# Feed-forward weights in 48 pieces, the first self-attention projections inside the feed-forward, and the gated weights' scaling kept at its place in the program

## The chip, the cores and the metric

The kernel runs on one core of a Trainium2 chip. Its time is the device time of one execution in microseconds (us). Engines are called PE (TensorE, matrix products), DVE (VectorE), ACT (ScalarE), POOL (GpSimd) and SP (SyncE, which here only issues DMAs). Each works through its own queue in order.

## The reference

A decoder of two layers over 16 sequences of 128 tokens with 512 features, every step followed by a residual sum and a layernorm. What matters here are the end of the first layer and the first half of the second:

```python
# end of layer 0: feed-forward with ternary weights (hidden size 2048)
xq = activation_quant(rms_norm(x))                      # rounded to 8 bit
p = silu(xq @ sign(W_g).T) * (xq @ sign(W_u).T)
x = layernorm(x + p @ sign(W_d).T)
# layer 1: self attention, all four products quantised (16 heads of 32, 4 key heads, rope, causal)
x = layernorm(x + bitlinear_attention(x))
# layer 1: gated cross attention on 128 context tokens
xn = rmsnorm(x) * norm_w
x = layernorm(x + sigmoid(xn @ wg.T) * (attention(xn @ wq.T, ctx) @ wo.T))
```

Before them come a state-space scan and a cross attention, behind them a mixture of experts.

## The kernel before

Five stages run one after the other in the source: `stage_ssm`, `stage_xattn`, `stage_ffn`, `stage_attention`, `stage_moe`. The tile framework traces them, orders the instructions of each engine by a priority (their place in the program) with a cost model of its own, and puts in the waits; an instruction can be issued far ahead of its place when its inputs and its buffer are there. `keep_in_program_order` forbids this for one instruction. Inside a stage the order is written by hand: helpers are generators, a list `running` holds those under way, and each step of a stage's loop advances each of them by one `yield`.

Large weights live in five slots of 16 KB per partition (`k.wslot`). In cross attention all five are full: two halves of wq, wk and wv together, two halves of wo (eight heads each).

`stage_xattn` loops over 128 units (16 sequences, 4 key groups, 2 halves). A unit makes scores, exponentials, transposes; `project(b)` runs eleven units ahead and uses the tiles `xT` and `cT`, two buffers each, 2 KB per partition. `prepare_first` quantises the feed-forward's first two sequences at the end.

`load_ffn_weights` is called where `stage_ffn` begins. For gate and up it brings two raw halves of 2 MB each into slots and takes their signs (ACT) into one bfloat16 slot; for down, two raw halves and two slots of signs.

`stage_ffn` takes two sequences at a time (`states`, eight of them). For a sequence and each quarter h of the hidden size it makes gate and up products, Silu (ACT), their product (DVE), a transpose, a split into a high and a low part (`hi`, `lo`) and eight products into `po`. `late`, `nxt` and `ahead` are generators advanced between: the last layernorm, the next two sequences' quantisation, and the preparation of attention's weights and masks (`load_bit_weights`, `load_gated_masks`).

`stage_attention` has 16 pairs of sequences, eight of `SelfAttention` and eight of `GatedAttention`, eight units each. A `SelfAttention` pair first runs `project()`, in twelve steps: `levels` (the rows' largest value, scaling, rounding, transposes), key and value product `pkv`, rope on keys (`kr`, whose addition and scaling run on POOL), query products `pq` and their rope (`qr`, addition on POOL), transposes. Pair 0's twelve steps and five of pair 1's are written ahead of the loop. In the loop, units run through scores, maximum (DVE), exponentials (ACT), row sums (`at_h`, `at_p` on POOL) and transposes.

`load_gated_weights` brings wq, wg, wo of the gated attention when `stage_attention` begins, waits eight steps, and multiplies the four chunks of wq and of wg by the norm's weights on POOL (line 870), a chunk every second step of the program.

Of the kernel before, what the change touches and what calls it, by code (L numbers as in the profile page):

```python
# [10 lines left out]
F32 = mybir.dt.float32  # L11
BF16 = mybir.dt.bfloat16
F32R = mybir.dt.float32r
# [7 lines left out]
P = 128  # L21
# [6 lines left out]

class Ctx:
    pass  # L30


class Side:
# [3 lines left out]
    def __init__(self, k):  # L37
        self.tc, self.n = k.tc, 0
# [375 lines left out]
def stage_xattn(k):  # L414
# [9 lines left out]
    with ExitStack() as ctx:  # L424
# [200 lines left out]

        def prepare_first():

            homes = {"xn": (wk, "m1", 4), "q_t": (wk, "m2", 2), "q_q": (wk, "sq", 2), "pt": (ppt, "pt", 2), "q_T": (k.early, "q_T0", 2)}
            st = k.ffn_first = Ctx()
            st.xs = k.x[0:2]  # L630

            def new(what, shape, dt):
                pool, tag, bufs = homes[what]
                return pool.tile(shape, dt, tag=tag, name=what, bufs=bufs)

            return prepare_ffn(k, st, new)

        def advance():
            for job in list(running):
                if next(job, running) is running:  # L640
                    running.remove(job)

        units = [(b, g, i) for b in range(NB) for g in range(G) for i in range(2)]
        running = [clear_rows(k, cst)]
        for t in range(-12, len(units) + 4):
            for lag, what in ((3, turn), (2, norm), (1, exps), (0, top), (-1, scores)):
                if not 0 <= t - lag < len(units):
                    continue
                b, g, i = units[t - lag]
                st = state[b]  # L650
                if what is scores and (g, i) == (0, 0):
                    st.b, st.sc, st.mx, st.pr, st.sm, st.pTs = b, {}, {}, {}, {}, {}
                what(st, g, i)
                if what is turn and i == 1:
                    running.append(outputs(st, g))
            if t == len(units) - 4:
                running.append(prepare_first())
            b, r = divmod(t + 11, U)
            if r == 0 and b < NB:
                running.append(project(b))  # L660
            b, r = divmod(t + 15, U)
            if t == -12 or r == 0 and b > 0 and b < NB and b % 4 == 0:
                running.append(angles(max(b, 0) // 4))
            advance()
# [1 line left out]
            advance()  # L666


def load_ffn_weights(k):

    nc, a = k.nc, k.args
    k.fw = []
    for name in ("ff_wgT", "ff_wuT"):
        wb = None
        for i in range(2):
            raw = k.wslot()
            nc.sync.dma_start(
                raw.rearrange("p (c e) -> p c e", c=2), a[name][i * 256 : (i + 1) * 256].rearrange("(c p) e -> p c e", p=P)
            )
            if wb is None:  # L680
                wb = k.wslot(BF16)
            for c in range(4):
                nc.scalar.activation(wb[:, i * 4096 + c * 1024 : i * 4096 + (c + 1) * 1024], raw[:, c * 1024 : (c + 1) * 1024], AF.Sign)
        k.fw.append(wb.rearrange("p (c e) -> p c e", c=KC))
    k.fd = []
    for i in range(2):
        raw = k.wslot()
        nc.sync.dma_start(
            raw.rearrange("p (h e) -> p h e", h=8), a["ff_wdT"][i * 1024 : (i + 1) * 1024].rearrange("(h p) e -> p h e", p=P)
        )  # L690
        fd = k.wslot(F32R)
        for c in range(4):
            nc.scalar.activation(fd[:, c * 1024 : (c + 1) * 1024], raw[:, c * 1024 : (c + 1) * 1024], AF.Sign)
        k.fd.append(fd.rearrange("p (h e) -> p h e", h=8))


def prepare_ffn(k, st, new):
# [31 lines left out]
def stage_ffn(k):  # L729
# [4 lines left out]
    with ExitStack() as ctx:  # L734
# [2 lines left out]
        pp = ctx.enter_context(tc.tile_pool(name="s3p", bufs=2, space=PSUM))  # L737
        po_ = ctx.enter_context(tc.tile_pool(name="s3o", bufs=1, space=PSUM))
        raws = ctx.enter_context(tc.tile_pool(name="s3r", bufs=1))
        load_ffn_weights(k)  # L740
        ahead = chain(load_bit_weights(k, raws, po_), load_gated_masks(k, raws))

        def prepare(st):
# [5 lines left out]
        def finish(st):  # L749
            layernorm(k, st.xs, st.xs)  # L750
            yield

        states = []
        for b0 in range(0, NB, 2):
            st = Ctx() if b0 else k.ffn_first
            st.xs = k.x[b0 : b0 + 2]
            states.append(st)
        late = iter(())
        for n, sn in enumerate(states):
            nxt = prepare(states[n + 1]) if n + 1 < len(states) else iter(())  # L760
            for i, x in enumerate(sn.xs):
                st = sn.step[:, i : i + 1]
                po = po_.tile([P, D], F32, tag="po", name="po")
                for h in range(HB):
                    ps = []
                    for w, tag in zip(k.fw, ("pg", "pu")):
                        p = pg.tile([P, D], F32, tag=tag, name=tag)
                        for c in range(KC):
                            nc.tensor.matmul(p, sn.qT[i][:, c], w[:, c, h * D : (h + 1) * D], start=c == 0, stop=c == KC - 1)
                        ps.append(p)  # L770
                    sg = wk.tile([P, D], F32, tag="sg", name="sg")
                    nc.scalar.activation(sg, ps[0], AF.Silu, scale=st)
                    nc.vector.scalar_tensor_tensor(sg, ps[1], st, sg, ALU.mult, ALU.mult)
                    pt = pp.tile([P, D], F32, tag="pt", name="pt")
                    transpose4(k, pt, sg)
                    hi = wk.tile([P, D], F32R, tag="hi", name="hi")
                    lo = wk.tile([P, D], F32R, tag="lo", name="lo")
                    nc.scalar.copy(hi, pt)
                    nc.vector.tensor_tensor(lo, pt, hi, ALU.subtract)
                    for part in (hi, lo):  # L780
                        for c in range(4):
                            hc = 4 * h + c
                            nc.tensor.matmul(
                                po, part[:, c * P : (c + 1) * P], k.fd[hc // 8][:, hc % 8],
                                start=part is hi and hc == 0, stop=part is lo and hc == 15,
                            )
                    next(late, None)
                    next(nxt, None)
                    if n and h >= 2:
                        next(ahead, None)  # L790
                nc.vector.tensor_tensor(x, po, x, ALU.add)
            late = finish(sn)
        for _ in late:
            pass


# [60 lines left out]
def load_gated_weights(k):  # L857

    nc, a, pool = k.nc, k.args, k.gated_pool
    W = k.gated_w = {}  # L860
    nw = pool.tile([P, KC], F32, name="nw")
    nc.sync.dma_start(nw, a["x2_nw"].rearrange("(c p) -> p c", p=P))
    for n in ("wq", "wg", "wo"):
        W[n] = pool.tile([P, KC, D], F32, name="x2_" + n)
        nc.sync.dma_start(W[n], a["x2_" + n + "T"].rearrange("(c p) e -> p c e", p=P))
    for _ in range(8):
        yield
    for n in ("wq", "wg"):
        for c in range(KC):
            nc.gpsimd.tensor_scalar(W[n][:, c], W[n][:, c], nw[:, c : c + 1], None, ALU.mult)  # L870
            yield
            yield


class SelfAttention:
# [8 lines left out]

    def __init__(self, k, p, pools):
        self.k, self.nc, self.xs = k, k.nc, k.x[2 * p : 2 * p + 2]
        self.wk, self.wr, self.pp, self.psc, self.ppt, self.pao = pools
        self.o, self.part, self.sT, self.s, self.sc, self.sc2, self.mx = [], [None, None], {}, {}, {}, {}, {}

    def rope(self, ps, n, tag):  # L890
        nc, HD, tabs = self.nc, self.HD, self.k.bit_tabs
# [198 lines left out]
class GatedAttention:  # L1090
# [15 lines left out]
    def project(self):  # L1106
# [5 lines left out]
            nc.sync.dma_start(self.kT[:, :, i * P : (i + 1) * P], k.x2_k[self.b0 + i])  # L1112
            nc.sync.dma_start(self.v[i], k.x2_v[self.b0 + i])
        ss = k.small.tile([P, 2], F32, tag="ss2", name="ss2")
        xT = wk.tile([P, KC, 2 * P], F32, tag="xT", name="xT")

        def turn(i):
            pt = self.pp.tile([P, D], F32, tag="pp", name="pt")
# [123 lines left out]
def stage_attention(k):  # L1242
# [6 lines left out]
    with ExitStack() as ctx:  # L1249
# [6 lines left out]
        pao = ctx.enter_context(tc.tile_pool(name="s4o", bufs=1, space=PSUM))  # L1256
        pools = wk, wr, pp, psc, ppt, pao
        pairs = [c(k, p, pools) for c in (SelfAttention, GatedAttention) for p in range(NB // 2)]
        units = [(pr, n) for pr in pairs for n in range(U)]

        begin = {}
        for m, pr in enumerate(pairs):
            begin.setdefault(U * m - (14 if m < NB // 2 else 10), []).append(pr)
        running = [load_gated_weights(k)]
        first = [pairs[0].project(), pairs[1].project()]
        for n in range(12):
            next(first[0])
            if n >= 7:
                next(first[1])
        running.append(first[1])  # L1270
        for t in range(-2, len(units) + 2):
            if k.moe:
                k.moe.tick()
# [41 lines left out]
class Moe:  # L1315
# [228 lines left out]
    def masks(self, u):  # L1544
        pm = self.pm.tile([P, D], F32, tag="pp" if self.pm is self.pp else "pm", name="pm")
        self.nc.tensor.matmul(pm, u.soft, self.mup[u.g], start=True, stop=True)  # L1546
        u.xg = self.wk.tile([P, D], F32, tag="xg", name="xg")
        self.nc.vector.tensor_tensor(u.xg, pm, u.row[:, 0:D], ALU.add)

    def turn_in(self, u):  # L1550
# [277 lines left out]
```

## Time and profile before

| | us |
|---|---|
| median of 3 runs (3319.4 to 3329.7) | 3327.35 |
| the profiled execution | 3324.17 |
| its span | 3322.3 |
| PE busy | 3145.9 |
| DVE busy | 1872.8 |
| ACT busy | 1379.3 |
| POOL busy | 1388.4 |

The span is what the profile covers; a few microseconds lie around it. Times in the views count from its start. Cross attention's last product ends at 1621.5 us, the feed-forward's last at 1901.4, the first scores of self attention are at 1926.8, and the experts begin behind 2440. An engine's busy time is the sum of its instructions' durations; a number in square brackets is the idle time of the engine ahead of a row, with what ended it.

### The profile page before, as it was taken

The page shows a single profiled execution, that of the slowest core. Times are in us where ns is not written, and L with a number is a line of the kernel's source. Part 1 is how long each engine was busy: PE and PEld are TensorE (multiplying, and loading weights), DVE is VectorE, ACT ScalarE, POOL GpSimd, SP SyncE. Part 2 cuts the span into 40 slices and gives each one's busy share as a digit, 9 for nine tenths or more (in the row PEclk, how much of TensorE's full clock was granted, in tenths as well). Part 3 has the DMA queues.
Part 4 walks back from the last instruction along what each step waited for, and adds up shares of the span by engine and source line. Part 5 has one row for each costly group of instructions (what it writes and reads, how often), then busy time and mean ns, then how long its engine had stood idle before and what let it go on. Part 6 is the DMA issues. An engine that isn't in the chain of part 4 may idle for free. (4 is left out here: it accounts for less than half of the span.)

```text
span 3322.3 us, 38519 instructions
## 1 busy us (share of the span) xinstructions
PE 3145.9 (95%) x12894; PEld 1811.7 (55%) x12944; DVE 1872.8 (56%) x4202; ACT 1379.3 (42%) x3299; POOL 1388.4 (42%) x1196
## 2 busy tenths in 40 slices
PE   6899998899999999999999989999999999999998
PEld 3444544455555555555566555666655566666665
DVE  5887878556556556556486669765553232233224
ACT  4655555233233233234433379865643231122221
POOL 6978887233333333332100066226624455333331
PEclk8999999999999999999999989999899999999999
DMA  7533332690000000001300010014435566555441
GB/s 235 134 81 97 85 85 69 227 310 8 7 4 4 7 4 4 7 0 76 112 1 1 29 36 1 11 58 150 149 115 185 193 222 210 167 180 175 160 160 62
DMA packets 162577, 317.29 MB, mean 96 GB/s; under 512 B 20233, under 2 KB 83209, under 8 KB 159300
## 3 DMA queue, kind: packets, MB, share of 16 engines
q1 hardware_dynamic: 124164, 216.23, 21.0%
q0 software_dynamic: 19200, 64.18, 5.6%
q10 hardware_dynamic: 19008, 34.35, 2.7%
q8 instruction: 105, 1.72, 0.2%
q14 instruction: 100, 0.82, 0.1%
HBM read 238.80 MB, written 129.04 MB: 111 GB/s over the span
## 5 line engine op out<-in xcount | busy, mean ns | idle before, releaser
L245 POOL TENSOR_TENSOR dBx<-dtx,BC 128x1024 f32<-128x1024 f32 x128 | 301.9, 2379 | 33.3 <-DVE h L258 26.0
L1562 PE MATMUL pg<-gu,xgT 128*128 128x352 f32 x784 | 299.4, 464 | 1.4 <-ACT act L1565 1.4
L1562 PE MATMUL pu<-gu,xgT 128*128 128x352 f32 x784 | 298.6, 463 | 0.1
L1566 DVE SCALAR_TENSOR_TENSOR act<-pu,row,act 128x352 f32<-128x352 f32 x98 | 57.1, 582 | 383.9 <-PE pu L1562 336.1
L1579 PE MATMUL y<-dn,aT 128*128 128x512 f32 x588 | 268.3, 592 | 0.0
L585 POOL TENSOR_TENSOR pr<-pr,sm 128x512 f32<-128x512 f32 x128 | 134.5, 1051 | 289.5 <-DVE sm L584 235.1
L236 ACT ACTIVATE h<-dt,negA 128x254 f32<-128x254 f32 x512 | 239.8, 474 | 14.9 <-DVE dt L178 2.1
L1605 POOL TENSOR_TENSOR x<-got,x 128x512 f32<-128x512 f32 x120 | 152.1, 1273 | 217.2 <-DMA got<-results,gidx 216.8
L616 PE MATMUL po<-w,aT 128*128 128x512 f32 x512 | 230.6, 593 | 0.5 <-DVE aT L610 0.5
L493 PE MATMUL pq<-w,xT 128*128 128x512 f32 x512 | 228.9, 594 | 0.0
L470 POOL TENSOR_TENSOR m<-m,m 128x512 f32<-128x512 f32 x96 | 121.4, 1265 | 245.3 <-DVE m L465 245.3
L1598 POOL DMA_INDIRECT got<-results,gidx x120 | 116.0, 966 | 253.0 <-DMA results<-yo 183.6
L578 ACT ACTIVATE pr<-sc,mx,sf 128x256 f32<-128x256 f32 x256 | 142.6, 561 | 188.1 <-DVE mx L571 175.8
L258 DVE TENSOR_TENSOR_SCAN h<-h,dBx 128x1024 f32<-128x1024 f32 x80 | 183.2, 2294 | 57.6 <-ACT h L236 43.0
L267 PE MATMUL py<-hC,ident 128*128 128x512 f32 x320 | 166.9, 650 | 41.2 <-ACT y L272 36.2
L1562 PEld LDWEIGHTS pu<-gu,xgT 128*128 128x128 f32 x784 | 150.3, 192 | 84.1 <-issue 2.4
L1562 PEld LDWEIGHTS pg<-gu,xgT 128*128 128x128 f32 x784 | 142.8, 192 | 65.8 <-issue 2.8
L1565 ACT ACTIVATE act<-pg 128x352 f32<-128x352 f32 x98 | 45.4, 464 | 299.6 <-PE pg L1562 278.6
L1579 PEld LDWEIGHTS y<-dn,aT 128*128 128x128 f32 x588 | 104.1, 190 | 100.8 <-issue 94.2
L1554 ACT COPY xgT<-ptx 128x512 f32<-128x512 f32 x98 | 57.3, 586 | 230.3 <-PE ptx L377 221.1
L1589 DVE COPY yo<-y 128x512 f32<-128x512 f32 x90 | 62.1, 690 | 156.7 <-PE y L1579 145.7
L493 PEld LDWEIGHTS pq<-w,xT 128*128 128x128 f32 x512 | 93.5, 190 | 102.0 <-issue 99.0
(363 smaller groups left out, 6830.5 us busy)
## 6 DMA issues: line engine op xcount, KB each, us to landing
bucket<-zeros SPq DMA_DIRECT2D x96, 388.0 KB, 8.2
row<-bucket SPq DMA_DIRECT2D x90, 388.0 KB, 3.5
BC<-bcd SPq DMA_DIRECT2D x128, 256.0 KB, 4.9
results<-yo ACTq DMA_DIRECT2D x90, 256.0 KB, 3.2
gu<-in_moe_guT SPq DMA_DIRECT2D x16, 1408.0 KB, 7.4
cT<-in_ctxT SPq DMA_DIRECT2D x32, 256.0 KB, 6.0
dn<-in_moe_downT SPq DMA_DIRECT2D x16, 512.0 KB, 6.8
rows<-r_row SPq DMA_DIRECT2D x16, 388.0 KB, 3.0
```

The costliest lines, as they stand in the source:

```text
L236: nc.scalar.activation(h[:, c, :, 1:], st.dt[:, c].rearrange("p (b t) -> p b t", b=BQ)[:, :, 1:], AF.Exp, scale=negA[:, c, n : n + 1])
L245: nc.gpsimd.tensor_tensor(dBx, st.dtx, BC[:, 0].unsqueeze(1).to_broadcast([P, KC, TQ]), ALU.mult)
L258: nc.vector.tensor_tensor_scan(hf, hf, df, 0.0, ALU.mult, ALU.add)
L267: nc.tensor.matmul(st.py[c], k.ident, st.hC[n][:, 2 * c : 2 * c + 2], start=n == 0, stop=n == NS - 1)
L470: nc.gpsimd.tensor_tensor(m1, m1, m2, ALU.add)
L493: nc.tensor.matmul(ps, src[:, c], w[c], start=c == 0, stop=c == KC - 1)
L578: nc.scalar.activation(pr[:, j], st.sc[g, i][:, j], AF.Exp, scale=st.sf[:, h : h + 1], bias=st.mx[g, i][:, j : j + 1], accum_out=sm[:, j : ...
L585: nc.gpsimd.tensor_tensor(pr, pr, sm.unsqueeze(2).to_broadcast([P, 2, 2 * P]), ALU.mult)
L616: nc.tensor.matmul(st.po, aT[:, j], k.wo[h // 8][:, h % 8], start=h == 0, stop=h == G * J - 1)
L1562: nc.tensor.matmul(ps, u.xT[:, c], gu[:, c, lo : lo + I], start=c == 0, stop=c == KC - 1)
L1579: self.nc.tensor.matmul(u.y, u.aT[:, c], u.w[1][:, c], start=c == 0, stop=c == 2)
L1605: nc.gpsimd.tensor_tensor(k.x[b], got, k.x[b], ALU.add)
```

## The change

Three things change.

1. `load_ffn_weights` becomes a generator and starts six units before the end of cross attention. It cuts the weights into 48 pieces of 128x512 (256 KB), in the order in which the feed-forward reads them: per quarter of the hidden size four pieces of gate and four of up, then sixteen of down. Raw pieces use the buffers of `xT` and `cT` in turn; four are fetched at first, each sign is followed by the fetch of one more, and a step takes five. The slot for the second half of down is asked for when its first piece comes.
2. Inside `stage_ffn` a generator `attention` runs the whole projection of pair 0 and five steps of pair 1's, one step per quarter from the second sequence of the seventh state, and one more in the last state. Its tiles borrow the feed-forward's buffers (`Homes`), and its PSUM tiles one bank, the `pp` tag of `po_`. What outlives the stage lies in `k.bit_pool` and `k.early`. `stage_attention` takes over the two pairs.
3. The scalings of the gated weights start sixteen steps into attention's loop instead of eight, and are kept in program order. The gated attention's `xT` gets one buffer instead of two, and so does `xg` in the two tiles of the experts that are opened early.

```diff
+            both = k.early.tile([P, 2, KC, P], BF16, tag="q_T", name="q_T")
+            return prepare_ffn(
+                k, st, lambda what, shape, dt: both[:, len(st.qT)] if what == "q_T" else homes.tile(shape, dt, what, what)
+            )
...
+        def ffn_weights():
+
+            return load_ffn_weights(
+                k, lambda n: wk.tile([P, D], F32, tag=("xT", "cT")[n % 2], name="w_raw"), lambda n: 5
+            )
...
+            if t == len(units) - 6:
+                running.append(ffn_weights())
...
-def load_ffn_weights(k):
+def load_ffn_weights(k, new, per):
...
+    k.fw = [k.wslot(BF16).rearrange("p (c e) -> p c e", c=KC) for _ in range(2)]
+    k.fd = [k.wslot(F32R).rearrange("p (h e) -> p h e", h=8)]
+    pieces = []
+    for e in range(4):
+        for name, w in zip(("ff_wgT", "ff_wuT"), k.fw):
+            for c in range(KC):
+                pieces.append((a[name][c * P : (c + 1) * P, e * D : (e + 1) * D], w[:, c, e * D : (e + 1) * D]))
+    for h in range(16):
+        pieces.append((a["ff_wdT"][h * P : (h + 1) * P], h))
+    raws = []
+
+    def fetch():
+        if len(raws) < len(pieces):
+            raws.append(new(len(raws)))
+            nc.sync.dma_start(raws[-1], pieces[len(raws) - 1][0])
+
+    for _ in range(4):
+        fetch()
+    yield
+    n = 0
+    while n < len(pieces):
+        for _ in range(per(n)):
+            if n == len(pieces):
+                break
+            to = pieces[n][1]
+            if isinstance(to, int):
+                if to == 8:
+                    k.fd.append(k.wslot(F32R).rearrange("p (h e) -> p h e", h=8))
+                to = k.fd[to // 8][:, to % 8]
+            nc.scalar.activation(to, raws[n], AF.Sign)
+            fetch()
+            n += 1
+        yield
...
-        load_ffn_weights(k)
...
+        def attention():
+
+            bit = k.bit_pool
+            homes = [
+                dict(q_t=(wk, "q_t", 3), q_q=(wk, "xn", 3), al=(bit, "al", 2), nal=(bit, "nal", 2)) for _ in range(2)
+            ]
+            homes[0].update(
+                q_T=(wk, "xn", 3), kr1=(wk, "q_q", 3), kr2=(wk, "q_T", 3), qr1=(wk, "xn", 3), qr2=(wk, "q_t", 3),
+                sv=(bit, "sv", 1), skT=(bit, "skT", 1), sqT=(bit, "sqT", 2),
+            )
+            homes[1].update(q_T=(k.early, "q_T", 1))
+            k.bit_first = [SelfAttention(k, p, (None, Homes(**h), Homes(pp=(po_, "pp", 1)), None, None, None)) for p, h in enumerate(homes)]
+            yield from k.bit_first[0].project()
+            k.bit_second = k.bit_first[1].project()
+            for _ in range(5):
+                next(k.bit_second)
+                yield
...
+                    if n == len(states) - 1:
+                        next(soon, None)
...
+                    if n + i >= len(states) - 1:
+                        assert next(ahead, None) is None
+                        next(soon, None)
...
-    for _ in range(8):
+    for _ in range(16):
...
-            nc.gpsimd.tensor_scalar(W[n][:, c], W[n][:, c], nw[:, c : c + 1], None, ALU.mult)
+            k.tc.keep_in_program_order(nc.gpsimd.tensor_scalar(W[n][:, c], W[n][:, c], nw[:, c : c + 1], None, ALU.mult))
...
-        xT = wk.tile([P, KC, 2 * P], F32, tag="xT", name="xT")
+        xT = wk.tile([P, KC, 2 * P], F32, tag="xT", name="xT", bufs=1)
...
+        pairs[0:2] = k.bit_first
+        for pr in pairs[0:2]:
+            pr.take(pools)
...
-        running = [load_gated_weights(k)]
-        first = [pairs[0].project(), pairs[1].project()]
-        for n in range(12):
-            next(first[0])
-            if n >= 7:
-                next(first[1])
-        running.append(first[1])
+        running = [load_gated_weights(k), k.bit_second]
...
-        u.xg = self.wk.tile([P, D], F32, tag="xg", name="xg")
+        u.xg = self.wk.tile([P, D], F32, tag="xg", name="xg", bufs=2 if self.depth > 2 else 1)
```

A class `Homes` gives a tile by its tag from the pool, tag and number of buffers named for it.

More of the change, by code (lines that the diff above doesn't have):

```diff
@@ L30, with __init__, tile @@
     pass
+class Homes:
+    def __init__(self, **homes):
+        self.homes = homes
+    def tile(self, shape, dt, tag, name, bufs=None):
+        pool, tag, bufs = self.homes[tag]
+        return pool.tile(shape, dt, tag=tag, name=name, bufs=bufs)
 class Side:
@@ L626, in prepare_first @@
         def prepare_first():
-            homes = {"xn": (wk, "m1", 4), "q_t": (wk, "m2", 2), "q_q": (wk, "sq", 2), "pt": (ppt, "pt", 2), "q_T": (k.early, "q_T0", 2)}
+            homes = Homes(xn=(wk, "m1", 4), q_t=(wk, "m2", 2), q_q=(wk, "sq", 2), pt=(ppt, "pt", 2))
             st = k.ffn_first = Ctx()
             st.xs = k.x[0:2]
[L632 to L636, printed above, removed]
+            both = k.early.tile([P, 2, KC, P], BF16, tag="q_T", name="q_T")
+            return prepare_ffn(
+                k, st, lambda what, shape, dt: both[:, len(st.qT)] if what == "q_T" else homes.tile(shape, dt, what, what)
+            )
         def advance():
@@ L666, in stage_xattn @@
             advance()
-def load_ffn_weights(k):
+def load_ffn_weights(k, new, per):
     nc, a = k.nc, k.args
[L672 to L694, printed above, removed]
+    k.fw = [k.wslot(BF16).rearrange("p (c e) -> p c e", c=KC) for _ in range(2)]
[29 more added lines that the diff above has]
+        yield
 def prepare_ffn(k, st, new):
@@ L757, in stage_ffn @@
             states.append(st)
-        late = iter(())
+        late, soon = iter(()), attention()
         for n, sn in enumerate(states):
@@ L793, in stage_ffn @@
         for _ in late:
+            pass
+        for _ in soon:
             pass
@@ L886, in __init__, with take @@
         self.k, self.nc, self.xs = k, k.nc, k.x[2 * p : 2 * p + 2]
+        self.take(pools)
+        self.o, self.part, self.sT, self.s, self.sc, self.sc2, self.mx = [], [None, None], {}, {}, {}, {}, {}
+    def take(self, pools):
         self.wk, self.wr, self.pp, self.psc, self.ppt, self.pao = pools
-        self.o, self.part, self.sT, self.s, self.sc, self.sc2, self.mx = [], [None, None], {}, {}, {}, {}, {}
     def rope(self, ps, n, tag):
```

## The prediction

> **What bounds the kernel now.** I read the row of slices first (TensorE, PE, is busy 95% of 3322.3 us, so only stretches where PE is not full can be won), then the tables of busy time by stretch around the three stages touched, then the timeline inside the two stretches that stand out. The chain of waits doesn't help: it reaches back only to 2553 us, behind everything that the change touches. In these rows the columns are the stretch, its length, and busy time of PE, weight loads, VectorE (DVE), ScalarE (ACT) and GpSimd (POOL), then PE's granted clock.
>
> ```profile
> PE   6899998899999999999999989999999999999998
> PEclk8999999999999999999999989999899999999999
> 1600.00:1620.00 20.00, 19.95 (x61) 9.32 (x61) 3.43 (x6) 6.25 (x11) 1.04 (x1) 1.00 0.47 167
> 1620.00:1640.00 20.00, 15.18 (x63) 8.94 (x64) 13.32 (x46) 11.40 (x15) 1.25 (x4) 0.91 0.47 162
> 1640.00:1660.00 20.00, 19.83 (x99) 12.33 (x99) 7.71 (x12) 5.95 (x10) 0.00 (x0) 1.00 0.00 1
> 1901.40:1926.80 25.40, 11.00 (x47) 5.49 (x47) 11.63 (x48) 7.07 (x12) 16.86 (x13) 0.65 0.63 208
> 1980.00:2000.00 20.00, 18.77 (x162) 12.21 (x164) 19.96 (x59) 19.01 (x47) 11.49 (x18) 1.00 0.00 1
> ```
>
> PE is full in cross attention (to 1621.5) and in the feed-forward (1640 to 1901), and has two holes: some 5 us where the feed-forward begins, and 1901.4 to 1926.8, where it does 11.0 us of work at 0.65 of the clock. Behind the second hole the limit changes: at 1980 DVE has no idle time left and ACT hardly any. What holds the first hole:
>
> ```profile
> 1622.43 3.90 ACT L693 ACTIVATE w<-w 128x1024 fp32r<-128x1024 f32 x4 [9.19 <-DMA w<-in_ff_wdT]
> 1626.35 1.28 ACT L772 ACT_TABLE_LOAD   x1
> 1628.38 0.59 PE L769 MATMUL pg<-w,q_T 128*128 128x512 bf16 x2 [4.51 <-ACT sg L772]
> ```
>
> ACT's queue stands 9.19 us for the last 2 MB of weights, takes their signs, loads the Silu table, and only then the Silu comes for which PE has waited 4.51 us. The second hole is a chain through POOL:
>
> ```profile
> 1907.99 6.40 POOL L870 TENSOR_SCALAR x_wq<-x_wq,nw 128x512 f32<-128x512 f32 x4 [284.68 <-DVE x L72]
> 1914.36 0.71 POOL L962 TENSOR_TENSOR kr<-kr,kr 128x256 f32<-128x256 f32 x1
> 1915.06 1.55 POOL L870 TENSOR_SCALAR x_wg<-x_wg,nw 128x512 f32<-128x512 f32 x1
> 1916.60 1.17 POOL L964 TENSOR_SCALAR kr<-kr,al 128x128 f32<-128x128 f32 x2
> 1917.76 3.09 POOL L870 TENSOR_SCALAR x_wg<-x_wg,nw 128x512 f32<-128x512 f32 x2
> 1920.83 1.25 POOL L899 TENSOR_TENSOR qr<-qr,qr 128x512 f32<-128x512 f32 x1
> 1922.07 1.55 POOL L870 TENSOR_SCALAR x_wg<-x_wg,nw 128x512 f32<-128x512 f32 x1
> 1923.60 1.25 POOL L899 TENSOR_TENSOR qr<-qr,qr 128x512 f32<-128x512 f32 x1
> 1928.92 1.23 DVE L1017 TENSOR_REDUCE mx<-sc 128x8 f32<-128x1024 f32 x1 [15.03 <-PE sc L1011]
> ```
>
> Eight scalings of the gated weights (6.40 + 1.55 + 3.09 + 1.55 = 12.6 us) stand in POOL's queue between the rope additions of pair 0, whose transposes PE needs for the first scores at 1926.8. DVE then has stood idle 15.03 us.
>
> **Part 1: weights in 48 pieces.** Removed: six 2 MB transfers and 24 signs of 128x1024 (4 x 3.9 us in fours, so 0.98 each in a row, 24 us). Added: 48 transfers of 256 KB and 48 signs of 128x512, at the 0.57 us of an ACT copy of that size, 27 us. So ACT gets 3 us more, inside cross attention's tail, where it was busy 38.5 of 66 us (1556 to 1622). SP gets 42 more issues of some 0.4 us; nothing else is queued on SP there. The raw pieces use the two buffers each of xT and cT, four in flight; the last reader of xT, the query product of sequence 15, is at 1557, and the weight slots come free then too, so about 44 pieces remain after 1557. A lone 256 KB load of cT lands in 2.6 us:
>
> ```profile
> cT<-in_ctxT SPq DMA_DIRECT2D x7, 256.0 KB, 2.6
> ```
>
> One buffer's round is issue 0.4 + landing 2.6 + sign 0.57 = 3.6 us, four at once give a piece each 0.9 us, 40 pieces end near 1594. The last eight need the slot of the first half of wo, free at 1609 (before, ACT's sign there waits for that product too), and take two rounds, to about 1616: before the last product of cross attention at 1621.5, not at 1626.3. A rule speaks against small pieces: the Trainium skill, "DMA: Bandwidth & Descriptors", section "Bandwidth", asks for at least 1 MiB per transfer for 75% of the peak. One behind the other, 48 at 2.6 us would be 125 us and would end the loads near 1680, a loss of some 50 us. The rule is about a lone transfer; with four open the row gives 43 us, and I take the row. Gain: 4.5 us of wait, plus 1.6 us since the first transposes and products behind it ran at a low clock (2.23 for eight where two fours later take 0.66 each, 1.86 where 1.20 is usual), less 1 us for the start of the pipeline that stays: **-5 us** (0 to -6.5).
>
> **Part 2: pair 0's projection and five steps of pair 1's inside the feed-forward.** PE's work moves with it, into a stage where PE is full: quantised transposes 2 x 0.61, pkv 1.04, pq 2 x 1.04, ptk 0.38, query transposes 2 x 0.66: 6.0 us longer. DVE (19.7 of 41.4 us from 1860), ACT (12.0) and POOL (0) have room for the rest. All its PSUM products pass through one bank, so a product can stand in PE's queue for the copy of the one before; with two steps per 4 us unit I take 1.5 us (0 to 6: 12 steps by half a copy). Then the first scores follow the last product directly, 1 us behind: -25.4 + 6.0 + 1.5 + 1.0 = -16.9. What does not move, about 4.7 us of DVE's 11.6 in the hole (the last layernorm, other pairs' q_t), now falls into the start of attention; before, DVE was idle 9.7 of 33.2 us from 1926.8 to 1960, so most of it finds room: +1. The full clock at that start (0.73 and 0.68 before, up to 1940): -1.
>
> **Part 3: the scalings in their written place.** Eight POOL instructions of 1.55 us go out of the hole (already counted) to steps 14 to 28 of self attention, about 2.9 us a step, so 40 to 85 us behind its begin, well ahead of their first reader, 160 us behind it. POOL has 8 us free of 20 there. But this is where DVE is full. The rows nearest:
>
> ```profile
> 1908.30 0.85 DVE L917 TENSOR_SCALAR q_t<-x,qs 128x512 f32<-128x512 f32 x1
> 1913.41 0.48 DVE L917 TENSOR_SCALAR q_t<-x,qs 128x512 f32<-128x512 f32 x1
> ```
>
> Both ran beside a scaling; one lost 0.37, the other nothing. The Trainium skill, "SBUF — State Buffer", section "SBUF: two separate sides", says that POOL and a DVE instruction with two ports or two SBUF inputs lock each other out for a whole instruction. At its worst that is 8 x 1.55 = 12.4 us of a full DVE, by the row 8 x 0.2 = 1.5 us. I take 2 (0 to 12.4), near the row, as several DVE operations can hit one scaling. One buffer less for the gated xT (its next writer comes more than one step after the last reader) and for the two early xg tiles: +0.5 (0 to 2).
>
> **Sum**: -5 - 16.9 + 1 - 1 + 2 + 0.5 = -19.4. The profiled execution took 3324.17 us, so 3304.8; it stands 3.2 below the median of the runs, 3327.35. I say **3305**.
>
> **Rivals.** (a) As summed, 3297 to 3314: 0.56. (b) More: no bank stalls, no lock, PE at full clock through the start: 3290 to 3297: 0.09. (c) The hole is given back inside self attention: the scalings at the full lock (+10.4) and bank stalls at 6 us (+4.5) leave -4.5: 3320. For it: DVE full at 1980, short DVE operations there last up to 1.2 us instead of 0.2. Against: POOL's scaling beside q_t cost little. 0.20. (d) The other side: ACT, in order, stands for each small piece. Without signs ACT has 18.3 us of work from 1556 to 1622, with 44 new ones 43.4; 22.6 us are free, 0.5 us a piece. Each wait beyond this moves the exponentials, and PE with them. By the rounds above a piece comes 0.3 us after ACT could take it; if landings with four open grow to some 5 us, the wait is about 1.1 us, 48 - 22.6 = 26 us lost, part 1's 5 too: 3324 - 14 + 26 = 3336; at 1.3 us a piece 3345. It decides from about 1.1 us on. For it: the old signs stood 2.65, 3.1 and 9.2 us for transfers. 0.15.
>
> Of 0.3% (10 us, what a measurement of this kernel can tell from no change): faster takes (a), (b) and a fifth of (c), less a little of (a)'s edge, 0.67; slower takes most of (d), 0.14; the rest is 0.19. The range from 3292 to 3336 leaves out about 1 in 10 on each side; the likeliest case alone is 3297 to 3314.
>
> **What would show it.** Part 1: no wait of a Silu behind a sign, PE over 19 of 20 us where the feed-forward begins, the last sign before cross attention's last product. Part 2: the feed-forward about 6 us longer, first scores 1 to 2 us behind its last product, clock 1.00 there. Part 3: scalings one by one between at_h additions, DVE's short operations no longer than before. Wrong, if ACT waits for pieces in cross attention's tail by more than 20 us in all, or if self attention lasts over 10 us longer from first to last scores.

## The result, and the profile after

The changed kernel takes 3312.39 us (median of 7 runs, 3306.72 to 3314.52), beside 3327.7 us for the kernel before on the same chip (7 runs, 3318.45 to 3336.66): 0.9956 of the time, with a 95% interval of 0.9941 to 0.9971. That is 15.3 us less, where 22 less than the first median, or 19.4 less than the profiled execution, were forecast. The profiled execution of after took 3313.51 us, 10.7 less than that of before.

Where the time went is read from landmarks: the last product of cross attention, the last of the feed-forward, the first and last scores of self attention, the first and last down products of the experts. A landmark is the start of its instruction. Between them lie these stretches, in us; the last two rows are kernels of the next section.

| kernel | first maximum of cross attention to its last product | to the feed-forward's last | to the first scores | self attention, first to last scores | gated attention, first to last scores | experts' down products | last of these to the end |
|---|---|---|---|---|---|---|---|
| before | 957.9 | 280.0 | 25.7 | 180.9 | 318.7 | 835.8 | 11.8 |
| after | 960.5 | 278.1 | 0.8 | 185.2 | 321.8 | 837.2 | 13.7 |
| after, old loader | 958.0 | 286.1 | 0.8 | 185.1 | 321.8 | 837.4 | 11.8 |
| after, no scalings | 963.0 | 278.1 | 0.8 | 180.5 | 319.1 | 837.4 | 13.7 |

In the four stretches that the change touches up to the last scores of self attention, after gains 2.6 - 1.9 - 24.9 + 4.3 = -19.9 us; 1.9 of it go at the very end. Of the 10.6 us by which the two spans differ, the remaining +7.4 lie where the change moves no work: 1.3 ahead of cross attention, 3.1 in gated attention, 1.6 from there to the first down product, 1.4 in the experts. Gated attention differs by as much between kernels that are alike in it (319.1 in the last row, against 321.8), so one pair of profiled executions is a poor measure of the gain.

The stretches where PE was not full, in the table of busy time by stretch of after (the columns are those of the prediction's rows):

```profile
1560.00:1580.00 20.00, 16.83 (x66) 9.83 (x63) 17.93 (x64) 13.92 (x32) 4.41 (x4) 1.00 0.71 225
1580.00:1600.00 20.00, 19.90 (x66) 11.17 (x67) 10.10 (x30) 17.73 (x46) 5.25 (x6) 1.00 0.69 213
1600.00:1620.00 20.00, 19.88 (x71) 10.24 (x70) 5.96 (x12) 8.99 (x19) 2.04 (x2) 1.00 0.30 93
1620.00:1640.00 20.00, 19.97 (x88) 11.20 (x87) 14.14 (x48) 7.04 (x11) 1.26 (x4) 1.00 0.46 146
1900.00:1920.00 20.00, 17.21 (x129) 10.74 (x127) 16.64 (x49) 12.93 (x30) 9.39 (x13) 1.00 0.78 248
1920.00:1940.00 20.00, 19.13 (x154) 11.64 (x154) 15.42 (x31) 18.79 (x48) 13.53 (x21) 1.00 0.05 17
```

The feed-forward's begin (1620 to 1640) is full, at 19.97 us where before had 15.18, and the second hole has gone: from 1900 to 1940 PE works 36.3 of 40 us at full clock. A new, small hole is in the first row. The timeline there, first PE's rows with idle time and then some of ACT's:

```profile
1569.16 0.66 PE L604 MATMUL pT<-ident,pr 128*128 128x128 f32 x4 [1.61 <-DVE pTs L609]
1580.10 3.70 PE L627 MATMUL po<-w,aT 128*128 128x512 f32 x8 [1.66 <-DVE aT L621]
...
1565.53 2.19 ACT L719 ACTIVATE w<-w_raw 128x512 bf16<-128x512 f32 x4 [0.96 <-DMA w_raw<-in_ff_wgT]
1569.26 0.63 ACT L719 ACTIVATE w<-w_raw 128x512 bf16<-128x512 f32 x1 [1.54 <-DMA w_raw<-in_ff_wuT]
1570.15 0.63 ACT L719 ACTIVATE w<-w_raw 128x512 bf16<-128x512 f32 x1 [0.26 <-DMA w_raw<-in_ff_wuT]
1571.63 0.58 ACT L589 ACTIVATE pr<-sc,mx,sf 128x256 f32<-128x256 f32 x1
```

ACT, in order, takes signs, stands for pieces that have not landed, and only then comes to the exponentials. DVE's row for the reciprocal of their sums, in the groups from 1555 to 1625 us, shows who waits longer there; first the row of before, then that of after:

```profile
L584 DVE RECIPROCAL sm<-sm 128x2 f32<-128x2 f32 x11 | 1.8, 161 | 6.2 <-ACT pr L578 6.1
```

```profile
L595 DVE RECIPROCAL sm<-sm 128x2 f32<-128x2 f32 x11 | 1.8, 164 | 9.8 <-ACT pr L589 9.8
```

The timeline of after where the feed-forward ends:

```profile
1902.44 1.10 PE L830 MATMUL po<-w,lo 128*128 128x512 f32 x4
1903.38 0.12 PEld L1062 LDWEIGHTS <-identb 128*128 128x128 bf16 x2 [0.28 <-issue]
1903.38 0.60 PE L1062 MATMUL sc<-mask,identb 128*128 128x512 bf16 x2
...
1903.92 1.16 PE L1066 MATMUL sc<-skT,sqT 32*128 32x128 f32 x16
```

Last product, mask and first scores follow each other without a wait.

### The profile page after: what moved, and what is told of

It reads as the page before. It is cut to its first block, busy times and chain, and to the rows that moved or that the text cites. A ratio compares the mean times of both kernels' runs of the same rounds, so it can differ in the third digit from the quotient of the medians.

```text
span 3311.7 us, 38679 instructions
## 1 busy us (share of the span) xinstructions
PE 3146.4 (95%) x12944; PEld 1809.6 (55%) x12944; DVE 1880.7 (57%) x4202; ACT 1382.5 (42%) x3323; POOL 1390.7 (42%) x1196
```

## The experiments

Ten kernels were run, each in five rounds with the kernel before on the same chip. In the texts on record, the theories have letters; each is said there. Two questions were open. What are the small pieces worth, and what does the loss in cross attention's tail (the stretch behind its last query product) come from? And why is self attention 4.3 us longer: the scalings' hold on DVE, which the prediction had at 2 us, or work that had used the hole and is now DVE's backlog?

| kernel | median us (of before) | ratio, 95% interval |
|---|---|---|
| pieces | 3324.91 (3324.42) | 0.9998 [0.9987, 1.0008] |
| nopieces | 3314.59 (3324.42) | 0.9963 [0.9950, 0.9975] |
| noscale | 3305.71 (3324.42) | 0.9939 [0.9926, 0.9952] |
| fold | 3309.28 (3324.42) | 0.9949 [0.9936, 0.9962] |
| hoist | 3322.8 (3325.72) | 0.9990 [0.9982, 0.9999] |
| double | 3316.42 (3325.72) | 0.9972 [0.9964, 0.9981] |
| seven | 3316.36 (3325.72) | 0.9973 [0.9961, 0.9985] |
| foldseven | 3310.31 (3325.72) | 0.9955 [0.9942, 0.9968] |
| foldold | 3309.03 (3322.75) | 0.9956 [0.9944, 0.9967] |
| foldper3 | 3304.13 (3322.75) | 0.9944 [0.9931, 0.9957] |

**The pieces alone, and all but the pieces.** "pieces" is the kernel before with part 1 of the change alone; "nopieces" is the kernel after with the loader of before, called where it was.

```diff
-            if t == len(units) - 6:
-                running.append(ffn_weights())
...
+        load_ffn_weights(k)
```

> The kernel before with the weights in 48 pieces alone. Theory A (the pieces close the hole at the feed-forward's begin, but the signs' waits for pieces delay the exponentials in cross attention's tail): cross attention's last product 2 to 4 us later than before, no wait of PE for the first Silu, the feed-forward's last product 3 to 6 us earlier, total 3321 to 3325. Rival B (the tail takes all of it back): feed-forward's last product where it was, total 3327 to 3329.

> The changed kernel with the old loader (2 MB transfers where the feed-forward begins); projections inside the feed-forward and the scalings in their place stay. Theory A: cross attention ends as in the kernel before (1621 to 1622), the hole of 4 to 5 us at the feed-forward's begin is back, and the total is 3 to 5 us over the changed kernel, 3315 to 3318. Rival B: total as the changed kernel, 3312.

Alone, the pieces change nothing that can be measured (0.9998). The stages show two effects of them. From the last query product of cross attention to the feed-forward's last product, pieces takes 340.8 us and before 345.2, so 4.4 us are gained; the time from the experts' last down product to the end grows from 11.8 to 13.6. The difference of nopieces and after says the same: 278.1 for 286.1 in the feed-forward, 960.5 for 958.0 ahead of it, 13.7 for 11.8 at the end. What is left, some 3 us, is less than the interval of a ratio tells apart, and the median of nopieces, 3314.59, falls between theory A's 3315 to 3318 and rival B's 3312.

**The scalings left out, and moved to another engine.** "noscale" leaves out the eight scalings, so the norm's weights are missing from its result. "fold" computes all of it: DVE's copies of the transposed activations out of PSUM become multiplications by the norm's weights, and nothing is left for POOL.

```diff
-            k.tc.keep_in_program_order(nc.gpsimd.tensor_scalar(W[n][:, c], W[n][:, c], nw[:, c : c + 1], None, ALU.mult))
...
-        nc.vector.tensor_copy(xT[:, :, 0:P], pt.rearrange("p (c t) -> p c t", c=KC))
+        nc.vector.tensor_tensor(xT[:, :, 0:P], pt.rearrange("p (c t) -> p c t", c=KC), k.gated_nw.unsqueeze(2).to_broadcast([P, KC, P]), ALU.mult)
```

> The changed kernel without the scaling of wq and wg by the norm's weights (that factor is left out of the result). Self attention from first to last scores takes 185.2 us in the changed kernel and 180.9 before. Theory L (the scalings on POOL hold DVE's short operations while DVE is full): it falls to 180 to 182, total about 3308. Rival G (the extra is the DVE work that the hole used to take: last layernorm, other pairs' rounding): it stays at 184 to 185, total 3311 to 3312.

> The changed kernel, but the norm's weights are multiplied into the transposed activations, in the DVE instruction that copies them out of PSUM (a copy of 128x512 becomes a product of the same size), so the eight POOL scalings go. Theory L: as without scalings, self attention 180 to 182 us, the 16 DVE instructions cost nothing (0.69 us either way), total about 3308, the fastest so far. Theory G: 184 to 185 us, total 3311 to 3312.

Self attention shrinks from 185.2 us to 180.5 and 180.3: the whole loss goes with the scalings. DVE's groups from first to last scores show how. In after:

```profile
L1073 DVE TENSOR_SCALAR mx<-mx,nal 128x8 f32<-128x8 f32 x31 | 14.5, 469 | 0.1
L972 DVE TENSOR_SCALAR q_t<-x,qs 128x512 f32<-128x512 f32 x12 | 7.2, 626 | 0.3 <-ACT q_q L976 0.3
L68 DVE SCALAR_TENSOR_TENSOR rs_t<-rs_t,rs_a 128x2 f32<-128x2 f32 x27 | 5.8, 227 | 0.0
L69 DVE SCALAR_TENSOR_TENSOR rs_y<-rs_t,rs_y 128x2 f32<-128x2 f32 x27 | 4.8, 188 | 0.0
```

The same groups in noscale:

```profile
L1068 DVE TENSOR_SCALAR mx<-mx,nal 128x8 f32<-128x8 f32 x31 | 11.5, 370 | 0.1
L967 DVE TENSOR_SCALAR q_t<-x,qs 128x512 f32<-128x512 f32 x12 | 6.2, 539 | 0.4 <-ACT q_q L971 0.3
L68 DVE SCALAR_TENSOR_TENSOR rs_t<-rs_t,rs_a 128x2 f32<-128x2 f32 x27 | 4.8, 187 | 0.0
L69 DVE SCALAR_TENSOR_TENSOR rs_y<-rs_t,rs_y 128x2 f32<-128x2 f32 x27 | 3.9, 157 | 0.0
```

Equal counts, and these four groups alone are 3.0 + 1.0 + 1.0 + 0.9 = 5.9 us longer with the scalings than without; the maximum over the scores (1206 and 1205 ns) and the largest values of so (664 in both) are not. DVE's sum in the stretch is 172.58 us against 167.31, and its idle time 12.6 against 13.2, so what was added is work of DVE and no wait. Other kernels repeat it: with the eight scalings (after, nopieces, seven) the stretch takes 185.1 to 185.2 us and DVE is busy for 172.5 to 172.6; without them (noscale, fold, foldold, foldper3) it takes 180.1 to 180.5, with 167.3 to 167.9. One kernel without scalings, foldseven, takes 182.5: DVE is busy there for 168.1 and idle for 14.4, at a mean granted clock of 0.98 where fold has 1.00. The clock is 0.98 in after too, but DVE's idle time there is that of fold (12.4), so the clock is not where the 4.7 us lie. One place, in the timeline of after:

```profile
1947.43 1.57 POOL L922 TENSOR_SCALAR x_wq<-x_wq,nw 128x512 f32<-128x512 f32 x1
...
1946.23 1.23 DVE L1072 TENSOR_REDUCE mx<-sc 128x8 f32<-128x1024 f32 x1 [0.36 <-PE sc L1066]
1947.49 0.66 DVE L1073 TENSOR_SCALAR mx<-mx,nal 128x8 f32<-128x8 f32 x1
```

and the same operations in noscale:

```profile
1944.78 1.22 DVE L1067 TENSOR_REDUCE mx<-sc 128x8 f32<-128x1024 f32 x1 [0.36 <-PE sc L1061]
1946.03 0.23 DVE L1068 TENSOR_SCALAR mx<-mx,nal 128x8 f32<-128x8 f32 x1
```

An operation on 8 columns took 0.66 us instead of 0.23 while the scaling ran. It ended at 1948.15, 0.85 us before the scaling did, so it was held for a part of the scaling only. What fold pays for its multiplications, the row of DVE's writes of xT, in after and then in fold (duration in ns, least, median and most):

```profile
L1182 DVE COPY xT<-pt x8: 669/680/685, 2068.5 to 2359.9; 128x512 f32<-128x512 f32 x8
```

```profile
L1177 DVE TENSOR_TENSOR xT<-pt,nw x8: 671/679/684, 2061.9 to 2347.5; 128x512 f32<-128x512 f32 x8
```

Nothing: 679 ns against 680. The product out of PSUM costs what the copy cost. In the whole time neither kernel is apart from the changed one (0.9939 and 0.9949, against 0.9956 [0.9941, 0.9971]); the gain is seen in the stage alone.

**Twice the scalings.** "double" follows each scaling by a second of the same form, by a tile of ones.

```diff
+            k.tc.keep_in_program_order(nc.gpsimd.tensor_scalar(W[n][:, c], W[n][:, c], one[:, c : c + 1], None, ALU.mult))
```

> The kernel after with each scaling followed by a second one of the same form, by a tile of ones: sixteen POOL instructions of 1.55 us in self attention in place of eight. Theory L (each scaling lengthens DVE's operations beside it by some 0.6 us of a full DVE): first to last scores 185.2 + 4.7 = 190 us, median 3316 to 3319. Rival C (the 4.7 us that go with the scalings are the half-rate stretch of PE that comes and goes, not the scalings): first to last scores 185 us, give or take 2.

Self attention takes 191.2 us, near theory L's 190, but not by theory L's cause. None, eight and sixteen scalings give 180.5, 185.2 and 191.2 us, with DVE busy for 167.3, 172.6 and 174.2: the first eight add 5.3 us to DVE's work, the second eight only 1.6, and DVE's idle time grows from 12.6 to 17.1. Two of DVE's groups show it, first in after, then in double:

```profile
L1073 DVE TENSOR_SCALAR mx<-mx,nal 128x8 f32<-128x8 f32 x31 | 14.5, 469 | 0.1
L1119 DVE TENSOR_REDUCE sm<-at_p 128x16 f32<-128x512 f32 x15 | 10.1, 676 | 5.0 <-POOL at_p L1086 5.0
```

```profile
L1076 DVE TENSOR_SCALAR mx<-mx,nal 128x8 f32<-128x8 f32 x31 | 13.4, 434 | 0.1
L1122 DVE TENSOR_REDUCE sm<-at_p 128x16 f32<-128x512 f32 x15 | 10.2, 678 | 9.9 <-POOL at_p L1089 9.9
```

The operation on 8 columns is no slower than with eight scalings. DVE waits 4.9 us longer for POOL's row sums, which now stand behind two scalings in POOL's queue. So most of the second 6.0 us is that queue, and that 191.2 came near 190 is luck. The price of the hold is read from the first eight alone: 0.6 us of the stage for a scaling of 1.56 us. Rival C, as it was written (185 us, give or take 2), falls.

**Part 3 undone.** "hoist" is the kernel after with the scalings in their old form: after eight steps, free in the order.

```diff
-    for _ in range(16):
+    for _ in range(8):
...
-            k.tc.keep_in_program_order(nc.gpsimd.tensor_scalar(W[n][:, c], W[n][:, c], nw[:, c : c + 1], None, ALU.mult))
+            nc.gpsimd.tensor_scalar(W[n][:, c], W[n][:, c], nw[:, c : c + 1], None, ALU.mult)
```

> The kernel after with part 3 alone undone: the eight scalings are free in the order again, and the order now puts them into POOL's queue from pair 1's rope addition and the first at_h on. Theory L (a scaling costs where it runs beside a full DVE, or where something in POOL's queue stands behind it): DVE has more room in the first 40 us of self attention, so self attention's lock cost shrinks, but the first scaling waits for the last layernorm and pair 1's rope and the first at_h stand behind it; first to last scores 183 to 190 us (after 185.2), median 3310 to 3318. Rival N (the written place was needed: the hole comes back): last product of the feed-forward to first scores, or the start of self attention, longer by 8 to 12 us, median 3320 to 3325.

Rival N holds: self attention takes 196.5 us, and nearly all of the gain is gone (0.9990). POOL's queue, and PE's row behind it, in the timeline of hoist:

```profile
1911.04 1.82 POOL L922 TENSOR_SCALAR x_wq<-x_wq,nw 128x512 f32<-128x512 f32 x1 [30.99 <-PE pts L388]
1912.83 0.71 POOL L1017 TENSOR_TENSOR kr<-kr,kr 128x256 f32<-128x256 f32 x1
...
1924.64 4.63 POOL L922 TENSOR_SCALAR x_wg<-x_wg,nw 128x512 f32<-128x512 f32 x3
1929.25 1.25 POOL L954 TENSOR_TENSOR qr<-qr,qr 128x512 f32<-128x512 f32 x1
...
1930.56 0.69 PE L388 MATMUL pt<-ident,qr 128*128 128x128 f32 x2 [8.44 <-POOL qr L954]
```

The same chain as in before, a pair later: the scalings now stand ahead of pair 1's rope. PE waits 8.44 us for it, and from 1920 to 1940 it is busy 11.09 us at 0.50 of the clock. So moving the scalings is what makes part 2 pay; whether the later start or the kept order does it, this run, which undoes both, doesn't tell.

**More pieces open, or fewer signs a step.** "seven" opens seven raw pieces, three in the free buffers of qT; "foldseven" does so on top of fold; "foldper3" takes three signs a step on top of fold; "foldold" is fold with the old loader.

```diff
-                k, lambda n: wk.tile([P, D], F32, tag=("xT", "cT")[n % 2], name="w_raw"), lambda n: 5
+                k, lambda n: wk.tile([P, D], F32, tag=("xT", "cT", "qT", "qT", "xT", "cT", "qT")[n % 7], name="w_raw", bufs=(2, 2, 7, 7, 2, 2, 7)[n % 7]), lambda n: 5
...
-    for _ in range(4):
+    for _ in range(7):
         fetch()
```

```diff
-                k, lambda n: wk.tile([P, D], F32, tag=("xT", "cT")[n % 2], name="w_raw"), lambda n: 5
+                k, lambda n: wk.tile([P, D], F32, tag=("xT", "cT")[n % 2], name="w_raw"), lambda n: 3
```

> The kernel after with seven raw pieces open in place of four, three of them in the free buffers of qT. Theory W (in cross attention's tail the signs stand for pieces that have not landed, and the exponentials behind them in ACT's queue come late): ACT's wait for pieces in the tail falls from some 10 us to under 4, first max to cross attention's last product 958 to 959 us (after 960.5, with the old loader 958.0), feed-forward unchanged at 278, median 3310 to 3312. Rival S (the signs' own 26 us on ACT delay the exponentials, whatever the loads do): waits fall but the tail stays at 960 to 961, median as after.

> The norm's weights multiplied in DVE's copy of the transposed activations (no scalings on POOL), and seven raw pieces open. If both effects add, self attention 180.4 us from first to last scores and cross attention's tail at 958 to 959: median 3306 to 3309 (folded alone 3309.3), ratio 0.994 to 0.995. Rival S: no better than folded alone.

> The kernel after with the norm's weights multiplied in DVE's copy (no scalings on POOL) and the weights in six large transfers as before. Theory Z (the small pieces are worth nothing over the whole run: they save some 8 us at the feed-forward's start, lose 2.5 to 4 us in cross attention's tail and 2 us at the end): median within 3 us of folded with pieces, 3307 to 3312; tail 958.0, feed-forward 286, end 11.8 us. Rival P (the pieces bring 4 us or more): median 3313 to 3316.

> The norm's weights multiplied in DVE's copy, and three signs a step in place of five, so that they are spread over 16 steps of cross attention's tail and the feed-forward's begin in place of 10. Theory S (in the tail ACT's queue is too densely filled with signs for the exponentials to come in time): first max to cross attention's last product 958 to 960 us (with five a step 962.6), but the last signs fall behind the tail's end, so the feed-forward's begin may give back up to 5 us; tail and feed-forward together 1236 to 1240 (with five 1240.6), median 3306 to 3310. Rival T (the loss in the tail is not ACT's): tail at 962 or more.

PE's idle time in the tail, from the last query product to cross attention's last product, is the length of that stretch less PE's busy time in it:

| kernels | idle us |
|---|---|
| before, nopieces, foldold (old loader) | 1.0, 1.0, 0.9 |
| after, pieces, double, hoist, fold, noscale (pieces, four open, five a step) | 3.4, 3.9, 4.2, 5.2, 4.0, 4.3 |
| seven, foldseven (seven open) | 4.1, 6.1 |
| foldper3 (four open, three a step) | 3.1 |

The pieces cost 2 to 5 us of idle time there. In noscale, fold, seven and foldseven PE is also busy 1.6 us longer in the tail, which has a stretch at a lower clock (0.98 in the mean over it in fold, 1.00 in after), so that by its length the tail loses 2.2 us (foldper3) to 6.8 us (foldseven) against the old loader. Kernels that are alike in the tail scatter by 2 us, so that theory S is not settled by foldper3's 3.1, nor by its 960.1 us from the first maximum on and 1238.2 us with the feed-forward, which both fall about where theory S had them. Theory W is not borne out: with seven open, ACT's wait for transfers in the tail falls only from 10.2 to 8.1 us, not to under 4, and PE's idle time does not fall at all. The wait of DVE's reciprocal behind the exponentials, 9.8 us in after, is 12.4 in seven. foldseven misses its expectation on both counts: 964.6 us where 958 to 959 were expected, and self attention 182.5 us where 180.4 were. So more open pieces are no cure. That the signs and their waits delay the exponentials is read from the timeline and not shown by a run; one in which the pieces have all landed before the tail was not made.

foldold and fold are equal within their intervals (0.9956 and 0.9949), as theory Z had it. The best median, 3304.13 us, is foldper3's; its ratio of 0.9944 [0.9931, 0.9957] is not apart from fold's, and neither interval is apart from that of the changed kernel.

## Why the prediction was right, and where its terms were off

The total holds: 3305 was said, 3312.4 measured, inside the likeliest case's own 3297 to 3314. The mechanism holds too, as the second hole, which carries most of the sum, closed as forecast. Taken apart, several terms were off, and they lie on both sides: in the stretches they come to some -16.4 us where -19.4 was said, and that the errors cancel so far is luck.

- **Part 1** (-5 said). The hole at the feed-forward's begin closed for more than was said: 7.4 us (280.0 to 272.6, before and pieces) to 8 us (286.1 to 278.1, nopieces and after), where the wait and the slow restart behind it had been put at 6. The sum had no term for a loss in the tail, and there the stage grew by 2.5 us. It looks like a weak form of rival (d): ACT waits 10.2 us for pieces in all, and exponentials stand behind these waits. That is less than the 22.6 us that the prediction counted as free on ACT, and than the 20 us of its sign of failure: room as a total over the tail did not say whether the exponentials come in time. (In rival (d) a landing of 5 us makes a wait of 0.9 us by its own round, not 1.1.) Signs 5 to 40 came at 1.2 us each where 0.9 was said. The last sign ended at 1620.3 us, before cross attention's last product, as forecast (1616 was said). Then 1.9 us at the end of the program came that nothing in the prediction names. What is left is -2.5 to -3.6, and alone the pieces could not be told from no change. Between the rule of the Trainium skill ("DMA: Bandwidth & Descriptors", section "Bandwidth"), that transfers be of at least 1 MiB, read as one piece behind the other, and the row of 2.6 us with four open, the row was the nearer guide: the loads ended in the tail, not near 1680. That the rule is about a lone transfer was the prediction's own reading.
- **Part 2** (-16.9 said). The gap went from 25.7 to 0.8 us (1.0 said), and the feed-forward grew by 6.1 (nopieces against before) or 5.5 (after against pieces), about the moved products' 6.0: the 1.5 us for stalls at the one PSUM bank did not come. PE's waits of over 0.15 us in the last 43 us of the feed-forward are 0.5 us in after and 0.7 in before. Together -18.8 to -19.4.
- **Backlog and clock** (+1 and -1 said). With the scalings out of the way (fold) self attention takes 180.3 us where before took 180.9. The backlog is there, as DVE is busy for 167.9 us where before had 163.8, and it finds room, as forecast: DVE's idle time falls from 17.1 to 12.4. What the clock (1.00, before 0.98) gave beside it these runs don't tell.
- **Part 3** (+2 said, 0 to 12.4). This term was mis-sized: 4.7 us. The row chosen for it, q_t beside a scaling in the hole, was taken where DVE had idle time to hide in, and two cases of it were made to stand for all of DVE's operations. The rule of the Trainium skill ("SBUF — State Buffer", section "SBUF: two separate sides") has the direction right, as the operations on 8 columns grew from 370 to 469 ns in the mean. But a hold over the whole of each scaling would have been 12.4 us, and the truth lay at 38% of it: the operation of 1947.49 ended 0.85 us before the scaling beside it. What the prediction asked as a sign (short operations no longer than before) was not met, while its bound for failure, self attention over 10 us longer, was not reached.
- **Buffers** (+0.5 said, 0 to 2). From the last scores of gated attention to the first down product of the experts, where the two early xg tiles are used, the kernels with one buffer take 43.7 to 44.2 us, before and pieces 42.1 and 41.4. Some 2 us may be the buffer's; it was not tried by itself, as the space of the second is taken.

Part 3 was weighed only as a cost. Hoist shows that the gain hangs on it: without it the scalings would have moved the second hole from pair 0 to pair 1, 11.3 us of self attention. The prediction took it for granted that they go out of the way, and did not price the case in which they don't.

The end has a trace of its cause. Every kernel with pieces takes 13.0 to 13.7 us from the last down product to the end of the span, every kernel with the old loader 11.8. DVE's chain there is the same instruction by instruction. The difference is a pause on SP, in the row of semaphore instructions that closes the program: 1.7 to 2.0 us with four pieces open, 1.2 us in seven and foldseven. Its place among the closing instructions differs between these two groups, but counted from the start it is always the same, ahead of the 1024th instruction of SP that the profile holds. The kernels with pieces have 1034 or 1042 of them, those with the old loader 955 or 956, so they never reach it. What SP does in the pause is not shown, and no run was made that cuts its instructions.

## What to carry to other kernels

Before work is moved into a stage that has room, look at what each engine's queue then holds next: removing the wait of pair 0 was worth next to nothing until the eight scalings were also taken from in front of pair 1. The cheapest place for a scaling is an instruction that moves the data anyway; here a multiplication on the way out of PSUM cost 679 ns where the copy had cost 680, and self attention was 4.9 us shorter without the other engine's scalings beside it, though the whole time does not tell the two kernels apart. Small pieces in an in-order queue should be priced twice, for what they free at their end and for what stands behind each of them on the way; free time of the queue as a total (22.6 us here, with 10.2 us of waits) does not cover the second.

## What was not expected of the hardware

A POOL multiplication of 128x512 with two SBUF operands (one of them a column) holds up some of DVE's operations beside it, above all those on 2 and 8 columns and q_t from x, at 0.6 us of the stage for one of 1.56 us (eight of them, 185.2 against 180.5 us), whereas the maximum over 1024 columns read from PSUM and that over 512 read from SBUF keep their 1.2 and 0.66 us.

Gated attention, with the same PE instructions, took 316.2, 318.7, 321.8 and 324.9 us in fold, before, after and double, with PE busy for 290.2, 293.9, 296.3 and 299.4, while ACT's busy time stayed at 211.1 to 211.4. The mean granted clock was 0.93, 0.91, 0.92 and 0.89: lowest where it took longest and highest where it was shortest. The other kernels of this case fit in, with 0.91 to 0.92 and 318.6 to 321.8 us; only the middle pair goes the other way. So the steps of some 3 us go with the clock, and what sets the clock is open. In a comparison of two profiles such a stage must be set apart before a gain of a few microseconds is read off the spans.
